# Cross attention of a decoder layer: the output's weights loaded and split in sixteen single pieces instead of four groups of four

## The chip, the cores and the metric

The kernel runs on one core of a Trainium2 chip. The metric is the device time in microseconds (us). The kernel before has three runs: 1482.58, 1488.05 and 1488.45 us, median 1488.05. One more execution was profiled, with a span of 1484.0 us.

A core has five engines that work side by side, each with its own queue of instructions: TensorE (PE, matrix products; PEld is its weight load), VectorE (DVE), ScalarE (ACT), GpSimd (POOL) and SyncE (SP), which here issues most of the DMA transfers. An engine takes its instructions in order; where one waits, all behind it on that engine wait too. PE's clock can be throttled: the profile shows the granted clock, 1.00 at full speed.

## The reference, cut to what matters

A decoder layer for 16 batches of 100 tokens, width 512, in float32:

```
x = layernorm(x + self_attention(x))                 # 16 heads, causal
x = layernorm(x + cross_attention(x, ctx))           # the change lies here
x = layernorm(x + moe(x))                            # top 2 of 8 experts, projection, rms norm

# cross attention: 16 heads of 128, 4 heads of keys and values, 361 encoder tokens a batch
q = rmsnorm((x @ Wq + bq) by heads) * qn_w
k = rmsnorm((ctx @ Wk + bk) by heads) * kn_w         # each serves four heads of q
v = (ctx @ Wv + bv) by heads
p = softmax(q k^T / sqrt(128) + mask)
cross_attention = (p v, heads side by side) @ Wo     # Wo: 2048 x 512
```

## The kernel before

**Pairs.** Every float32 array that enters a product is held as a pair, a high part [...] and a low part, the rest. `split` (L120 to L127) makes one: a cast of the high part on ACT (L124) and a subtraction of the low part on DVE or POOL (L127). `mm3` (L129 to L133) is one product of pairs in three matmuls, whose lines L131, L132 and L133 appear in the profile for all products.

**Weights.** The arena `WH`, `WL` has eight slots of 512x512 pairs. `load_unit` (L194) fills one through `split_rows` (L185 to L190): for each of four pieces of 128x512 (256 KB) it takes a stage tile (a ring of three, tag `f`), issues a DMA on SP that is kept in program order, casts on ACT and subtracts on POOL. The output's weights Wo take four slots (`wo_slot = (3, 7, 0, 4)`), one for each group of four heads, in tiles that the profile calls `f_wo`; they are first used with the last batch, by `d_part`.

**The stages.** Self attention in groups of four batches; a stage that makes the queries of the cross attention and writes them to DRAM (`qd`); the cross attention; its output product with the router; the experts, with tokens sorted by expert into tiles, gathered by indirect DMAs (`xs`, a ring of five), transposed on PE (`pte`), multiplied, and written back (`ysd`).

**The cross attention's loop.** It runs over 64 items, a batch b and a group of heads g, in the order b*4 + g. An item of group g does, in the program's order:
- for g = 0, 1, 2 the keys' and values' products of one chunk of the next batch's encoder tokens (`kv_project`: `pk`, `ks`, `pv`), and the split of the next chunk of the encoder tokens (`cf` to `cT`);
- `x_load` of the queries of the item after next (`qf`, on SP; split by ACT and POOL);
- for g = 1, 2, 3 the transposes of a chunk of the next batch's keys (`kv_turn`: `ptk`, `kT`);
- in turn: the next item's four heads of scores (`x_scores`: product `s`, bias and maximum on DVE, the exponential `p` on ACT, the sum's inverse on DVE, the scaling of `p` on POOL), the three transposes of its own probabilities (`x_turn`: `ptp`, split into `pT_h` by ACT and `pT_l` by DVE), and the products with the values (`x_attend`: `av`), the third of them one item late;
- behind the last of these, the output `o` of the item before on ACT (L720) and its write to DRAM (`od`, L725, on SP).

At the end of the items with g = 1 of batches 2, 5, 8 and 11 stands one `load_unit` of Wo, four pieces in a row:

```python
        if g == 1 and b in (2, 5, 8, 11):
            load_unit(f"wo_{b // 3}", wo_slot[b // 3], Wo4[b // 3])
```

**What sets the order.** The program is built in a tile context with a planner that simulates a timeline and orders each engine's instructions by it, so they do not follow the program's text strictly; DMAs marked with `keep_in_program_order` keep theirs among each other. An edit in one place can so move instructions in another.

Of the kernel before, what the change touches and what calls it, by code (L numbers as in the profile page):

```python
# [17 lines left out]
B, S, D = 16, 100, 512  # batches, tokens of a batch, model width  # L18
T = B * S
KC = D // 128  # chunks of the model width  # L20
NH = 16  # heads of both attentions
HD1 = D // NH  # head width of the self attention
SE = 361  # encoder tokens of a batch
SP = SE + 1  # the same, even
NKV, HD2 = 4, 128  # key/value heads and head width of the cross attention
GR = NH // NKV
CH = [(0, 128), (128, 128), (256, SE - 256)]  # chunks of the encoder tokens
NE = 8  # experts
GB = 4  # batches of a token group
NG = B // GB  # L30
GT = GB * S
TT = [(t, min(128, T - t)) for t in range(0, T, 128)]  # tiles of all tokens
# [5 lines left out]
def pieces(t0, n):  # L38
    """The batches that tokens t0 to t0 + n lie in: (batch, its token, offset, count)."""
    out, t = [], t0  # L40
    while t < t0 + n:
        b, r = divmod(t, S)
        m = min(S - r, t0 + n - t)
        out.append((b, r, t - t0, m))
        t += m
    return out


class Pair:
    """A float32 array as the exact sum of two that float32r holds."""  # L50
# [12 lines left out]
def tile_decoder_layer(  # L63
# [29 lines left out]
    # Exp and Ln of one table serve both attentions.  # L93
# [26 lines left out]
    def split(dst, src, high=None, low=None):  # L120
        """dst, a pair, from src."""
        high, low = high or nc.scalar, low or nc.vector
        if high is nc.scalar:
            nc.scalar.copy(dst.h, src)  # L124
        else:
            high.tensor_copy(dst.h, src)
        low.tensor_tensor(dst.l, src, dst.h.bitcast(FP), ALU.subtract)  # L127

    def mm3(out, a, b, start, stop):  # L129
        """The product of two pairs, to float32's accuracy."""  # L130
        nc.tensor.matmul(out, a.h, b.h, start=start, stop=False)  # L131
        nc.tensor.matmul(out, a.h, b.l, start=False, stop=False)  # L132
        nc.tensor.matmul(out, a.l, b.h, start=False, stop=stop)  # L133
# [5 lines left out]
    def rsqrt(v, p, n, name, p_=None):  # L139
        """1 / sqrt(v), from the activation tables, with one Newton step."""  # L140
# [33 lines left out]
    # Eight slots of 512 rows by 512 columns, each a pair: weights, and what fits  # L174
    # beside them.
# [6 lines left out]
    def slot_of(s):  # L182
        return Pair(WH[:, s], WL[:, s])

    def split_rows(dst, src, name, high=None, low=None):  # L185
        """Weights from DRAM into a pair, by rows."""
        for k in range(KC):
            f = stage.tile([128, D], FP, name=f"f_{name}_{k}", tag="f")
            tc.keep_in_program_order(nc.sync.dma_start(f, src[:, k]))
            split(dst[:, k], f, high, low or nc.gpsimd)  # L190
# [44 lines left out]
    def chunk(n, c, queue=None):  # L235
        """Weights from DRAM, 128 columns (of queries or keys) or rows (of values)."""
        cc = slice(c * 128, (c + 1) * 128)
        chunks.append(n)
        p, bufs = (w1, 2) if len(chunks) % 5 > 2 else (stage, 3)
        f = p.tile([128, KC, 128], FP, name=f"f_{n}_{c}", tag="f", bufs=bufs)  # L240
        if n == "v":
            f = f.rearrange("p k n -> p (k n)")
            part, dst = src[n][:, c], units["wv_s"][:, c]
        else:
            part, dst = src[n][:, :, cc], units[f"w{n}_s"][:, :, cc]
        (queue or nc.sync).dma_start(f, part)
        return dst, f
# [7 lines left out]
    # Keys of four heads, each in its own block of rows and of columns.  # L255
# [8 lines left out]
    # Added to negated scores: zero up to the diagonal, BIG past it.  # L264
# [35 lines left out]
    def self_q(g, c):  # L300
# [3 lines left out]
        # The scores come out negated and scaled.  # L304
# [71 lines left out]
    def self_attend(g, c, r):  # L376
# [3 lines left out]
        # Of each head's rows only its own columns are its output.  # L380
# [48 lines left out]
    LA = 3  # items that scores are ahead by  # L429
    extra = {}  # what comes with an item  # L430
# [77 lines left out]
    # Both norms' weights and the negated scale of the scores.  # L508
# [107 lines left out]
    # Six pairs of values and two of queries, in slots 1 and 5.  # L616
# [87 lines left out]
    def x_attend(b, g, i):  # L704
# [13 lines left out]
        # The weights of a token sum to one: the values' bias comes last.  # L718
# [27 lines left out]
    TAIL = 3  # tiles whose parts come by weights, not by tiles  # L746
# [12 lines left out]
    def d_part(i, among={}):  # L759
        """A part of the output's product; others' products are among its own."""  # L760
        t, g = parts[i]
        n = TT[t][1]
        if g == 0:
            # The scores' banks are free by the time that those of the first wait.
# [28 lines left out]
    HEAD = 1  # parts with a group of heads of the last batch  # L793
    d_i = ExitStack()
    for i, (b, g) in enumerate(order):
# [34 lines left out]
        if g == 1 and b in (2, 5, 8, 11):  # L830
            load_unit(f"wo_{b // 3}", wo_slot[b // 3], Wo4[b // 3])
# [13 lines left out]
    # Small products: logits, ranks, counts, tokens of slots, their experts.  # L845
# [30 lines left out]
    def d_logits(t):  # L876
        """The products of the router with a tile, to go among longer ones."""
# [15 lines left out]
    # An expert's tokens in order, 128 to a tile of slots. The tiles of slots come in  # L893
    # the order in which their first tokens do, but the first EARLY of those that the
    # tokens of the first CUT tiles fill come before the others.
    URGENT = 1000
    I32, HF = mybir.dt.int32, mybir.dt.float16
    NSL = NE + (2 * T - NE) // 128  # tiles of slots: enough for any choice
    CUT, EARLY = NT - 4, 11
    # At the cut at most NE - 1 tiles' worth of choices lies in tiles not full.  # L900
# [9 lines left out]
    # Whole numbers below 2 ** 11 are in float16 where products take them.  # L910
    # Expert numbers less NE, negative ones.
# [5 lines left out]
    # Ones where the partition's number comes before the column's.  # L917
# [11 lines left out]
    # lower[e, i] is one where i is less than e, on all partitions.  # L929
# [31 lines left out]
    def by_128(dst, src, name):  # L961
        """The whole part of src / 128."""
# [5 lines left out]
    def table(name, shape, dt=FP):  # L968
        """A table of shape, first after partitions the tiles."""
# [3 lines left out]
    def choose(a, b):  # L973
        """The two experts of each token of tiles a to b, and its ranks in them."""
# [4 lines left out]
        for j in range(2):  # L979
            # The largest value of each token, and the first place that has it.  # L980
# [19 lines left out]
        if b == NT:  # L1000
            # The last tile's tokens past the end choose none.
# [17 lines left out]
        if b in (CUT, NT):  # L1019
            # The choices that come before each tile of tokens.  # L1020
# [26 lines left out]
        # What the tokens give to their slots: the tile's expert, by its first slot,  # L1047
# [7 lines left out]
        # and their numbers.  # L1055
# [11 lines left out]
    def settle(a, b):  # L1067
        """The tiles of slots of the choices of tiles a to b."""
# [6 lines left out]
        # Tiles of slots that an expert has before each tile of tokens.  # L1075
# [4 lines left out]
        # One where it opens another.  # L1080
# [5 lines left out]
        def before_it(these, till, less, name):  # L1086
            """How many of these come before each."""
# [28 lines left out]
        # That one's place among all tiles of slots.  # L1116
        new = before_it(opn, opened, EARLY if a else 0, "new")
        if a == 0:
# [6 lines left out]
            # new less those of the first EARLY that come before it, negated,  # L1125
# [3 lines left out]
            # or first, if it is itself of those.  # L1129
# [6 lines left out]
        # The place of the one before it.  # L1136
# [7 lines left out]
        # The tile of slots of a choice, by its rank.  # L1144
# [18 lines left out]
    def slots(a, b, upto):  # L1163
        """Of tiles a to b of slots: the tokens, and where the weights lie."""
# [69 lines left out]
    early = [1, 2, 5, 6]  # slots that are free already  # L1234
# [117 lines left out]
    # Tiles of tokens from REST on come after the last product, from LATE on also  # L1352
    # the gathers for them.
    REST, LATE = 6, 8
    # When the tiles before LATE are turned to, by tiles of slots.
    TURN = (19, 20, 21, 22, 24, 26, 28, 30)
    BEHIND = 2  # products that the last norms come after

    def upto(t):
        """Tiles of slots among which are all that the tokens of tile t are in."""  # L1360
        # At most NE of the tiles so far are not full at the cut.
# [93 lines left out]
    # Roots taken together: of tiles in the first norm, of tiles in the second.  # L1455
# [16 lines left out]
    def root(j, t, of=V2):  # L1472
        """What to take the root of for tile t in norm j, or its reciprocal root."""
# [8 lines left out]
    def f_first(t):  # L1482
        """The first norm of tile t, and what the second takes."""
# [3 lines left out]
        # The first norm's result and x2, both times the root s: the second norm  # L1487
        # drops s, but for its share of v.
# [62 lines left out]
    def roots(v, m, name):  # L1551
        """Of v's first m columns the root of four times it, of the others 1 / sqrt."""
# [6 lines left out]
        # A Newton step for each.  # L1559
# [15 lines left out]
    def newton(v, name):  # L1575
        """1 / sqrt(v): from a guess by v's exponent, three Newton steps."""
# [130 lines left out]
```

## Time and profile before

| what | value |
|---|---|
| runs | 1482.58, 1488.05, 1488.45 us (median 1488.05) |
| profiled execution, span | 1484.0 us |
| mean granted clock of PE | 0.972 |
| PE, DVE, ACT, POOL busy | 94%, 69%, 55%, 49% |
| DMA, mean rate | 108 GB/s |
| loads of f_wo | 16, on SP at 582.8 to 949.4 us, to landing 2.6 / 4.6 / 5.9 us (min / median / max) |
| casts of f_wo on ACT (L124) | 16, median 622 ns; ACT waited for the DMA in 7 of them, 8.2 us |
| subtracts of f_wo on POOL (L127) | 16, median 1276 ns; POOL waited for ACT in 3 of them, 1.5 us |

How to read it: "busy" is the time in which an engine worked on an instruction. A line of a timeline has start, length (of a run of x instructions), engine, line of the kernel, operation, output<-input, shape, and in brackets how long the engine had been idle before it and what ended that. A line of a table of stretches has start:end and length, the busy time of PE, of its weight loads, of DVE, ACT and POOL with the counts of instructions, then the granted clock, the share of the DMA engines' time and GB/s. A batch's stretch is taken from its third-group score product to that of the next batch, which is a fixed place in the loop.

### The profile page before, as it was taken

The page shows a single profiled execution, that of the slowest core. Times are in us where ns is not written, and L with a number is a line of the kernel's source. Part 1 is how long each engine was busy: PE and PEld are TensorE (multiplying, and loading weights), DVE is VectorE, ACT ScalarE, POOL GpSimd, SP SyncE. Part 2 cuts the span into 40 slices and gives each one's busy share as a digit, 9 for nine tenths or more (in the row PEclk, how much of TensorE's full clock was granted, in tenths as well). Part 3 has the DMA queues.
Part 4 walks back from the last instruction along what each step waited for, and adds up shares of the span by engine and source line. Part 5 has one row for each costly group of instructions (what it writes and reads, how often), then busy time and mean ns, then how long its engine had stood idle before and what let it go on. Part 6 is the DMA issues. An engine that isn't in the chain of part 4 may idle for free.

```text
span 1484.0 us, 24770 instructions
## 1 busy us (share of the span) xinstructions
PE 1391.4 (94%) x7248; PEld 1139.8 (77%) x7248; DVE 1018.2 (69%) x3523; ACT 813.3 (55%) x2164; POOL 731.9 (49%) x853
## 2 busy tenths in 40 slices
PE   7999999999999999999999999999999898798985
PEld 6777786788877888788788788788887676576763
DVE  5775766677676777777777677677745558752698
ACT  5766877444444566566666566566654233332453
POOL 6455545534424555455655555555544444442643
PEclk9999999999999999999999999999999999899997
DMA  4011015456544222122322322321435645666774
GB/s 130 34 46 62 22 36 145 144 142 118 125 97 92 74 65 80 44 64 64 89 61 64 87 63 63 93 60 45 99 107 142 207 164 159 191 213 184 253 232 146
DMA packets 197875, 159.77 MB, mean 108 GB/s; under 512 B 133322, under 2 KB 152878, under 8 KB 197742
## 3 DMA queue, kind: packets, MB, share of 16 engines
q1 hardware_dynamic: 187904, 137.83, 33.7%
q0 software_dynamic: 4576, 14.95, 3.3%
q10 hardware_dynamic: 5262, 5.41, 1.3%
q8 instruction: 60, 0.98, 0.3%
q14 instruction: 73, 0.60, 0.1%
HBM read 107.16 MB, written 50.99 MB: 107 GB/s over the span
## 4 chain that ended last, share of the span: by engine, by line
PE 67%; DVE 17%; DMA 7%; issue 4%; ACT 3%; POOL 1%; SPq 1%; DVEq 0%; POOLq 0%; ACTq 0%
PE pv L131 4%; PE pv L132 4%; PE pv L133 4%; PE pq L131 4%; PE ptp L700 4%; PE pq L132 4%; PE pq L133 3%; PE s L131 3%; PE s L133 3%; PE s L132 3%; PE pk L131 3%; PE pk L133 3%; PE pk L132 3%; DVE ksq L639 2%; PE av L383 2%
## 5 line engine op out<-in xcount | busy, mean ns | idle before, releaser
L692 POOL TENSOR_SCALAR p<-p,sums 100x361 f32<-100x361 f32 x256 | 146.7, 577 | 107.7 <-DVE sums L691 88.7
L679 DVE CUSTOM_DVE_ANT_0 p<-s,nmask 100x361 f32<-100x361 f32 x256 | 133.5, 527 | 73.6 <-PE s L133 71.5
L690 ACT ACTIVATE p<-p,nm 100x361 f32<-100x361 f32 x256 | 153.4, 602 | 47.2 <-DVE nm L679 44.1
L127 DVE TENSOR_TENSOR pT_l<-ptp,pT_h 128x400 fp32r<-128x400 f32 (+1 forms) x192 | 107.4, 567 | 58.3 <-ACT pT_h L124 58.1
L124 ACT CAST pT_h<-ptp 128x400 fp32r<-128x400 f32 (+1 forms) x192 | 91.5, 488 | 33.4 <-PE ptp L700 32.8
L700 PE MATMUL ptp<-ident,p 100*128 100x100 f32 (+1 forms) x768 | 108.2, 253 | 0.1
L700 PEld LDWEIGHTS ptp<-ident,p 100*128 100x128 f32 (+1 forms) x768 | 95.9, 152 | 15.5 <-POOL p L692 4.2
L127 POOL TENSOR_TENSOR cT_l<-cf,cT_h 128x512 fp32r<-128x512 f32 (+1 forms) x48 | 54.4, 1134 | 97.2 <-ACT cT_h L124 95.9
L133 PE MATMUL acc<-WH,ot_l 128*128 128x512 f32 (+1 forms) x208 | 86.2, 415 | 8.4 <-DVE ot_l L127 5.4
L131 PE MATMUL acc<-WH,ot_h 128*128 128x512 f32 (+1 forms) x208 | 85.8, 413 | 3.5 <-ACT ot_h L124 3.5
L127 POOL TENSOR_TENSOR WL<-qf,WH 128x400 fp32r<-128x400 f32 x64 | 67.3, 1051 | 43.5 <-ACT WH L124 39.7
L131 PE MATMUL s<-kT_h,WH 128*100 128x362 f32 x256 | 88.7, 357 | 0.0
L131 PE MATMUL av<-pT_h,WH 128*128 128x400 f32 (+1 forms) x192 | 76.7, 400 | 8.2 <-ACT pT_h L124 8.2
L132 PE MATMUL acc<-WL,ot_h 128*128 128x512 f32 (+1 forms) x208 | 84.4, 406 | 0.0
L133 PE MATMUL s<-kT_h,WL 128*100 128x362 f32 x256 | 84.1, 329 | 0.0
L132 PE MATMUL s<-kT_l,WH 128*100 128x362 f32 x256 | 83.7, 327 | 0.0
L131 PE MATMUL pq<-WH 128*128 128x512 f32 (+1 forms) x208 | 82.3, 396 | 0.1
L132 PE MATMUL pq<-WL,WH 128*128 128x512 f32 (+1 forms) x208 | 81.6, 394 | 0.5 <-POOL WL L127 0.5
L551 POOL TENSOR_TENSOR qs<-qs,r_q 128x512 f32<-128x512 f32 (+1 forms) x52 | 54.3, 1075 | 54.5 <-DVE r_q L155 25.5
L131 PE MATMUL pv<-WH,cT_h 128*128 128x512 f32 (+1 forms) x192 | 80.3, 418 | 0.8 <-DVE WL L127 0.8
L639 DVE CUSTOM_DVE_ANT_0 ksq<-ks 128x128 f32<-128x128 f32 (+1 forms) x192 | 78.3, 408 | 2.4
L360 POOL TENSOR_TENSOR p<-p,rinv 100x400 f32<-100x400 f32 x64 | 54.2, 855 | 51.8 <-DVE rinv L359 37.3
(349 smaller groups left out, 4407.3 us busy)
## 6 DMA issues: line engine op xcount, KB each, us to landing
qf<-qd SPq DMA_DIRECT2D x64, 200.0 KB, 2.6
of<-od SPq DMA_DIRECT2D x48, 256.0 KB, 3.5
cf<-in_ctxT SPq DMA_DIRECT2D x16, 722.0 KB, 4.2
eb<-in_expert_b SPq DMA_DIRECT2D x32, 256.0 KB, 3.8
ysd<-xs SPq DMA_DIRECT2D x32, 256.0 KB, 4.1
f_e<-in_expert_w SPq DMA_DIRECT2D x30, 256.0 KB, 4.5
f_wq<-in_Wq SPq DMA_DIRECT2D x16, 256.0 KB, 4.0
f_wo<-in_Wo SPq DMA_DIRECT2D x16, 256.0 KB, 4.6
```

Of the source, the lines that this page charges most:

```text
L124: nc.scalar.copy(dst.h, src)
L127: low.tensor_tensor(dst.l, src, dst.h.bitcast(FP), ALU.subtract)
L131: nc.tensor.matmul(out, a.h, b.h, start=start, stop=False)
L132: nc.tensor.matmul(out, a.h, b.l, start=False, stop=False)
L133: nc.tensor.matmul(out, a.l, b.h, start=False, stop=stop)
L360: nc.gpsimd.tensor_tensor(p, p, rinv.unsqueeze(2).to_broadcast([S, 4, S]), ALU.mult)
L551: nc.gpsimd.tensor_tensor(qr[:, hs, :], qr[:, hs, :], rs[:n, hs].unsqueeze(2).to_broadcast([n, GR, HD2]), ALU.mult,)
L639: nc.vector.tensor_tensor_reduce(out=sq[:n], in0=kr[:, h, :], in1=kr[:, h, :], scale=1.0, scalar=0.0, op0=ALU.mult, op1=ALU.add, accum_out ...
L679: nc.vector.tensor_tensor_reduce(out=p, in0=sc[:, :SE], in1=nmask, scale=1.0, scalar=BIG, op0=ALU.add, op1=ALU.min, accum_out=nm,)
L690: nc.scalar.activation(p, p, AF.Exp, bias=nm, scale=-1.0, accum_out=sh)
L692: nc.gpsimd.tensor_scalar(p, p, sh, 1.0, ALU.mult, ALU.mult)
L700: nc.tensor.transpose(pt[:n, h, :], probs[h][:, c0 : c0 + n], ident[:S, :S])
```

## The change

The condition on g and b goes. A table `wo_rows` names sixteen items, every third one from item 8 to item 53, each with one piece m; a new function `load_row` does for one piece what `split_rows` does for four. m // 4 is the group of heads (the slot), m % 4 the piece in it. Item i is batch i // 4 with g = i % 4, so the pieces stand at g = 0, 3, 2, 1 in turn. The transfers, the casts and the subtracts are as many and as large as before.

```diff
     wo_slot = (3, 7, 0, 4)
+    wo_rows = {8 + 3 * m: m for m in range(NKV * KC)}
+
+    def load_row(name, src, slots_, m):
+        u, k = divmod(m, KC)
+        units[name] = slot_of(slots_[u])
+        f = stage.tile([128, D], FP, name=f"f_{name}_{k}", tag="f")
+        tc.keep_in_program_order(nc.sync.dma_start(f, src[u][:, k]))
+        split(units[name][:, k], f, nc.scalar, nc.gpsimd)
+
     for i, (b, g) in enumerate(order):
...
-        if g == 1 and b in (2, 5, 8, 11):
-            load_unit(f"wo_{b // 3}", wo_slot[b // 3], Wo4[b // 3])
+        if i in wo_rows:
+            load_row(f"wo_{wo_rows[i] // KC}", Wo4, wo_slot, wo_rows[i])
```

The rest of the diff takes out comments and docstrings. With the new places the planner also orders some instructions of the experts' stage differently: the products that count the tokens of each expert come one product later, and the transposes of several tiles of tokens (`pte`) and the gathers behind them come earlier. Lines behind the new function are ten further down.

## The prediction

> **What bounds the kernel now.** I read the page's shares of busy time first, then the cross attention cut at each batch's score product of its third group of heads (the table of stretches), then the chain of waits and each engine's timeline around one of the four loads. The page:
>
> ```profile
> span 1484.0 us, 24770 instructions
> PE 1391.4 (94%) x7248; PEld 1139.8 (77%) x7248; DVE 1018.2 (69%) x3523; ACT 813.3 (55%) x2164; POOL 731.9 (49%) x853
> ```
>
> TensorE sets the pace. The change lies in the cross attention, so what it can give is read there. Each row is start:end and length in us, the busy time of PE, weight loads, DVE, ACT and POOL with their counts, the granted clock, the DMA share and GB/s:
>
> ```profile
> 525.49:563.55 38.06, 37.81 (x219) 32.38 (x218) 28.46 (x109) 24.81 (x68) 19.73 (x28) 1.00 0.26 64
> 563.55:608.41 44.86, 41.48 (x220) 34.97 (x218) 30.85 (x110) 26.60 (x72) 24.69 (x32) 0.92 0.29 77
> 608.41:646.48 38.07, 37.82 (x219) 32.36 (x218) 28.48 (x110) 24.82 (x68) 19.73 (x28) 1.00 0.27 64
> 684.59:726.21 41.62, 38.45 (x219) 32.42 (x218) 30.66 (x109) 26.60 (x72) 24.66 (x32) 1.00 0.33 84
> 802.40:847.36 44.96, 41.52 (x219) 34.99 (x218) 30.43 (x109) 26.69 (x72) 24.68 (x32) 0.92 0.31 77
> 923.57:967.23 43.66, 40.00 (x219) 33.75 (x218) 30.34 (x109) 26.68 (x72) 24.72 (x32) 0.96 0.31 80
> ```
>
> A batch without a load takes 38.08 with PE 99% busy. The four with a load (4 more casts on ACT, 4 more subtracts on POOL: x68 to x72, x28 to x32) take 6.78, 3.54, 6.88 and 5.58 more: **22.8 us in all, the most that the change could take away here.** PE's own busy time grows where the clock is below 1. At half clock for 6.83, 0, 6.83 and 3.41 us (the lost clock times the length) half of that is lost: 8.5 us. The other 14.3 is plain waiting, about 3.6 a group, and the chain and the timelines show how it comes about:
>
> ```profile
> 581.82 0.91 SPq L725 DMA_DIRECT2D od<-o  x2
> 582.78 1.49 SPq L189 DMA_DIRECT2D f_wo<-in_Wo  x3
> ...
> 582.78 4.50 DMA f_wo<-in_Wo
> ...
> 587.30 0.62 ACT L124 CAST WH<-f_wo 128x512 fp32r<-128x512 f32 x1 [1.85 <-DMA f_wo<-in_Wo]
> ...
> 596.02 0.45 PE L132 MATMUL av<-pT_l,WH 128*128 128x400 f32 x1 [1.18 <-DVE pT_l L127]
> 598.07 0.57 PE L131 MATMUL av<-pT_h,WH 128*128 128x400 f32 x1 [1.06 <-ACT pT_h L124]
> ```
>
> The load is issued on SP directly behind the writes of o (od), which wait for the end of an item (a batch and a group of heads). It lands 4.5 us later, but ACT works in order and has its cast next, so it stands 1.85 us with everything behind it, then casts pieces between its exponentials; DVE and at last PE wait. The half clock begins some 0.5 us after these two gaps.
>
> **The change, part by part.** *The work is the same:* 16 loads, 16 casts at 622 ns, 16 subtracts at 1276 ns, now one of each with items 8, 11, ... 53. Nothing on PE is added. ACT is busy 25 of 38 us in a plain batch, POOL 20, SP less, so 16 x 0.62 = 10 us of ACT and 16 x 1.28 = 20 us of POOL have room on average; without that cover these sums would be the cost.
>
> *The wait of the first piece is not removed, it is had sixteen times.* In the changed order of instructions each load still stands directly behind the od writes, ahead of a load of queries (qf), on SP; each cast stands only some 3 us of ACT's work behind the same point. What I cost is one piece in a plain batch's timeline, put where the order has it. Landing is od's end plus 4.5 (first pieces of the four groups: 4.52, 4.26, 4.63, 4.62). Issuing a piece takes SP 0.43, by which qf is late; qf is for the item after next, so nothing waits. Behind the waiting cast on ACT are exponentials and pT_h; for these DVE (pT_l, ks) and then PE's av, ptp and pk wait. The four positions in a batch, four pieces each:
> - Items of g=0: ACT would reach the cast at 574.98, 695.55, 813.4, 935.0; the data land at 576.1, 696.6, 815.0, 936.15. With the cast, less the room before pk needs its bank: 0.8, 0.75, 1.3, 0.8 = 3.65.
> - g=3 (row below): od is issued at 641.94 to 642.85, the piece lands at 647.4; ACT is free at 645.19, so it stands 2.2 and casts 0.6. pT_h, due at 646.37, comes at about 648.5, and POOL's 1.28 lies ahead of the next p. PE loses about 2.2: x4 = 8.8.
> - g=2: two pieces ahead of the third pT_h, 1.35 and 1.9, two behind it, 0.7 each = 4.65.
> - g=1: reached at 668.2, 786.05, 907.16, 1027.1, landed at 669.7, 788.3, 909.2, 1028.6; less the room at pk: 0.3, 1.15, 0.9, 0.35 = 2.7.
>
> ```profile
> 641.94 0.91 SPq L725 DMA_DIRECT2D od<-o  x2
> ...
> 644.57 0.63 ACT L124 CAST cT_h<-cf 128x512 fp32r<-128x512 f32 x1 [0.29 <-PE pv L132]
> ...
> 646.37 0.47 ACT L124 CAST pT_h<-ptp 128x400 fp32r<-128x400 f32 x1
> ```
>
> Sum of waits: 19.8, against 14.3 before: **5.5 worse**. Bounds: 5 if the room downstream takes most of each (0.3 a piece), 29 if each costs the 1.8 that the first of a group stood.
>
> *The clock.* Before, groups cost 8.5 here. [...] gaps of 1.18 and 1.06 within 3 us were enough, in three of four groups. [...] by the row the six larger pieces (g=3 and two of g=2) are doubtful. At 1.7 a trip (half of 3.41) none to ten trips cost 0 to 17; I take two or three, 4, nearer the single gaps of before that tripped nothing (the 684.59 row at 1.00). **4.5 better.**
>
> [...] a DVE operation on 128x4 values took 1.28 alongside a subtract of f_wo:
>
> ```profile
> 595.88 1.28 DVE L171 TENSOR_SCALAR v_k<-kss 128x4 f32<-128x4 f32 x1
> ...
> 595.87 1.26 POOL L127 TENSOR_TENSOR WL<-f_wo,WH 128x512 fp32r<-128x512 f32 x1
> ```
>
> [...] DVE is 75% busy in a batch, and PE waits only where pT_l or ks is next. I keep it inside the waits above.
>
> *The experts' stage.* Nothing is edited there, but the planner orders it anew: the routing products go one product later, and the transposes of the tiles of tokens (pte), with the gathers behind them, several places sooner. Before, PE waits there on a ring of five gathered tiles:
>
> ```profile
> 1330.00:1350.00 20.00, 15.44 (x67) 11.90 (x66) 6.61 (x10) 5.68 (x10) 3.79 (x4) 0.91 0.67 212
> ...
> 1339.42 1.09 PE L1206 MATMUL pte<-ident,xs 128*128 128x128 f32 x4 [3.20 <-DMA xs<-x2d,idx]
> ...
> 1410.00:1430.00 20.00, 19.56 (x97) 15.51 (x96) 19.36 (x55) 9.06 (x18) 7.95 (x8) 1.00 0.86 256
> ```
>
> The first row has 4.6 us of PE idle and 0.9 of lost clock (9% of 20, halved); the gathers of tiles 13 to 15 come 3 to 5 us sooner in the new order, and later PE is 98% busy, so what is gained is kept. All of it would be 5.5, plus 2 for the wait at tile 19. I take **4 better**; from 8 better to 2 worse (the later routing products hold up the first tiles).
>
> Sum: +5.5 - 4.5 - 4 = -3 against the profiled 1484.0, so 1481 as a profile. The median of the runs is 1488.05, 4.05 above that span, and the three runs spread over 5.9, of which the profile lies in the lower part. Against the median the sum is **1485**.
>
> **The rivals.**
> 1. *Pieces trip the clock* (the other side). A wait of 2 us per piece halves the clock for a window or two, as a group does. Place: batches with a g=3 piece; price 3.4 (two windows) in each of four, and 1.7 in four more: 20 in place of 4, so 1485 + 16 = 1501. For it: three of four groups tripped. Against: they had two gaps over 1 and further ones. From 1495.5 - 1485 + 4 = 14.5 us of lost clock, some 8 windows, the kernel is measurably slower.
> 2. *PE's queue and the rooms absorb single pieces.* ACT's wait of 1 to 2 is made good before PE needs pT: 0.3 a piece, 5 in all, no trip: -14.3 + 5 - 8.5 = -18, with -4 elsewhere: 1466. For it: ACT is 35% free and its room returns with every item; the group at 684.59 cost only 3.54 for four. Against: PE has 0.25 us of idle time in 38, and pT is made just in time.
> 3. *Only the place moves*: pieces cost together what groups do (22.8), and the experts' stage gives nothing: 1488.
>
> **How the numbers follow.** A measurement tells about 0.5%, 7.4 us, from no change: 1480.6 to 1495.5 is the same. Chances: main case 0.40 (own range 1477 to 1492, its two unknowns being the clock 0 to 10 and the experts 0 to 8), rival 1 0.12, rival 2 0.30, rival 3 0.18. Faster: all of rival 2 and a third of the main case, 0.43; the bound's other side takes most of rival 1, 0.10. Same 0.47. The range 1465 to 1497 leaves out the far ends of rivals 1 and 2.
>
> **What would show it.** Right: ACT waits on f_wo in nearly all of 16 casts, together 20 us or more against 8.2 before (7 of 16); batches with a piece 39 to 41 long, g=3 ones the longest; granted clock at 1.00 in most; the wait before tile 13's transpose shorter. Wrong: batches of 38.1 to 38.5 throughout (rival 2), or four and more at 0.96 and below (rival 1).

## The result: 0.4% faster, and the profile after

The changed kernel takes 1479.28 us (median of six runs, 1472.23 to 1484.90) against 1485.53 for the kernel before beside it: a ratio of 0.9958, interval 0.9938 to 0.9979. On another chip the same pair gave 0.9981 (0.9963 to 0.9999). The forecast was 1485 with 1465 to 1497, and no change beyond 0.5% as the likeliest outcome. The time came out inside the range; the sum that led to it did not come out term by term, and that is what the experiments are about.

The page of the changed kernel, profiled execution:

```profile
span 1479.0 us, 24756 instructions
PE 1385.8 (94%) x7248; PEld 1135.1 (77%) x7248; DVE 1010.7 (68%) x3523; ACT 812.2 (55%) x2164; POOL 733.5 (50%) x853
```

Batches 2, 3, 4, 6, 9 and 12 of the cross attention, cut as before (start:end and length, busy time of PE, weight loads, DVE, ACT, POOL, granted clock, DMA share, GB/s):

```profile
562.98:601.01 38.03, 37.71 (x220) 32.44 (x218) 27.99 (x110) 24.30 (x66) 21.16 (x29) 1.00 0.31 77
601.01:642.86 41.85, 39.94 (x220) 33.82 (x218) 29.18 (x110) 26.49 (x72) 22.25 (x30) 0.96 0.28 64
642.86:681.45 38.59, 38.29 (x220) 32.53 (x218) 28.25 (x109) 25.12 (x69) 20.97 (x29) 1.00 0.29 69
719.47:759.45 39.98, 38.09 (x219) 32.36 (x218) 29.30 (x109) 26.23 (x72) 22.30 (x30) 1.00 0.27 68
836.01:881.38 45.37, 41.77 (x219) 34.97 (x218) 28.96 (x111) 26.59 (x72) 22.23 (x30) 0.92 0.24 60
957.89:1000.75 42.86, 40.32 (x219) 33.94 (x218) 29.03 (x111) 26.60 (x72) 22.23 (x30) 0.96 0.26 63
```

The cut is, put exactly, at the third score product of a batch's first group of heads, which PE makes during the item before. So a piece at the end of an item with g=3 falls into the next batch's stretch. Where four batches paid before, now twelve have a piece in them, and four of these (3, 6, 9, 12, the ones with a g=3 and a g=2 piece) pay nearly everything. Batches whose piece stands at g=0 (the first row) pay nothing.

The answer for the tile f_wo, and the three queues around the first piece at g=3:

```profile
L124 ACT CAST WH<-f_wo x16: 617/620/626, 575.7 to 1023.9; 128x512 fp32r<-128x512 f32 x16
...
  DMA f_wo<-in_Wo: 24.5, 16
```
```profile
597.90 0.50 SPq L800 DMA_DIRECT2D f_wo<-in_Wo  x1
...
601.89 0.62 ACT L124 CAST WH<-f_wo 128x512 fp32r<-128x512 f32 x1 [2.16 <-DMA f_wo<-in_Wo]
...
603.01 0.47 ACT L124 CAST pT_h<-ptp 128x400 fp32r<-128x400 f32 x1
...
603.53 0.45 PE L131 MATMUL av<-pT_h,WH 128*128 128x400 f32 x1 [1.28 <-ACT pT_h L124]
604.14 0.60 PE L132 MATMUL av<-pT_l,WH 128*128 128x400 f32 x1 [0.16 <-DVE pT_l L127]
```

Each of the sixteen casts makes ACT wait for its landing, 24.5 us in all (7 casts and 8.2 us before). At g=3 the cast comes just ahead of a pT_h, whose ptp PE had made by 601.23, and PE stands 1.28 and 0.16 us.

**An account for all runs.** The names are those of the experiments below. "Excess" is what batches 1 to 13 take over 38.08 us each. The trace shows the half clock (0.50) in stretches of 3.41 or 6.83 us, counted here as one or two windows; in before and after, matmuls of pv follow each other there at 0.43 us (median) in place of 0.23, and a window is counted as half of its length lost, 1.71. The rest of the excess is direct waiting. "Rest" is from batch 15's mark to the end of the execution. "Order" says which of the two orders of the experts' stage the build has.

| kernel | excess | half-clock windows (lost) | direct | ACT waited on f_wo | order | rest | ratio to before (95%) |
|---|---|---|---|---|---|---|---|
| before | 22.9 | 5 (8.5) | 14.4 | 8.2 | before | 390.7 | |
| after | 19.1 | 4 (6.8) | 12.3 | 24.5 | after | 390.1 | 0.9958 (0.9938-0.9979) |
| after_again | 18.6 | 3 (5.1) | 13.5 | 25.7 | after | 395.4 | 0.9981 (0.9963-0.9999) |
| early | 15.1 | 1 (1.7) | 13.4 | 24.6 | after | 395.3 | 0.9973 (0.9960-0.9987) |
| at01 | 17.7 | 4 (6.8) | 10.9 | 23.8 | before | 387.7 | 0.9980 (0.9958-1.0002) |
| at23 | 27.5 | 3 (5.1) | 22.4 | 29.4 | after | 393.7 | 1.0049 (1.0032-1.0066) |
| poolcast | 8.4 | 0 | 8.4 | 0 (POOL: 31.3) | after | 392.6 | one run |
| pin | 6.1 | 0 | 6.1 | 12.3 | near after | 391.7 | 0.9947 (0.9929-0.9965) |
| early_pin | 6.5 | 1 (1.7) | 4.8 | 0 | before | 392.3 | 0.9932 (0.9908-0.9955) |
| group_early | 19.2 | 6 (10.2) | 9.0 | 0.6 | before | 395.2 | 0.9996 (0.9980-1.0012) |
| group_dve | 4.8 | 0 | 4.8 | 0.4 | its own | 392.2 | 0.9908 (0.9876-0.9939) |
| before_dve | 11.6 | 2 (3.4) | 8.2 | 8.0 | after | 395.1 | 0.9939 (0.9918-0.9961) |
| after_dve | 19.3 | 2 (3.4) | 15.9 | 25.2 | after | 389.3 | 0.9985 (0.9961-1.0009) |
| best13 | 1.2 | 0 | 1.2 | 0 | before | 395.1 | 0.9866 (0.9835-0.9897) |

Excess and rest come from one profiled execution each, the ratios from up to twenty timed ones; the rest alone varies by 7.7 us over these executions. The two do not agree to the microsecond: against the kernel before, pin loses 16.8 us of excess and is timed 7.9 us faster, early_pin 16.4 and 10.1, group_dve 18.1 and 13.7, best13 21.7 and 20. The profiled execution of pin is the second fastest of 20 and that of early_pin the fastest of nine, so their excess may flatter them. Only the changed kernel was profiled twice (19.1 and 18.6).

### The profile page after: what moved, and what is told of

The parts are those of the page before. It is cut to its first block, busy times and chain, and to the rows that moved or that the text cites. A ratio compares the mean times of both kernels' runs of the same rounds, so it can differ in the third digit from the quotient of the medians.

```text
span 1479.0 us, 24756 instructions
## 1 busy us (share of the span) xinstructions
PE 1385.8 (94%) x7248; PEld 1135.1 (77%) x7248; DVE 1010.7 (68%) x3523; ACT 812.2 (55%) x2164; POOL 733.5 (50%) x853
## 5 line engine op out<-in xcount | busy, mean ns | idle before, releaser
L700 PEld LDWEIGHTS ptp<-ident,p 100*128 100x128 f32 (+1 forms) x768 | 95.6, 151 | 13.5 <-POOL p L692 2.3
L131 PE MATMUL pk<-WH,cT_h 128*128 128x512 f32 (+1 forms) x192 | 78.2, 407 | 0.2
```

The costliest lines, as they stand in the source:

```text
L700: nc.tensor.transpose(pt[:n, h, :], probs[h][:, c0 : c0 + n], ident[:S, :S])
```

## The experiments

**Is the wait for the landing what a piece costs?** First, the load one item earlier:

```diff
         if i in wo_rows:
-            load_row(...)                  # load, cast, subtract
+            split_row(wo_rows[i])          # cast, subtract
+        if i + 1 in wo_rows:
+            fetch_row(wo_rows[i + 1])      # load
```

> The changed kernel with one thing moved: the load of each piece is issued one item (6 to 14 us) before its cast; casts and subtracts stay at the same items, and the experts' stage has the changed kernel's order. Theory (the wait for the landing on ACT is what a piece costs): ACT waits on f_wo for less than 2 us in all (24.5 in the changed kernel), the batches' excess over 38.08 falls from 19.2 us to 0 to 3, no half clock in the cross attention, about 1462 us. Rival (the cast and the subtract themselves are in the way[...]): excess stays at 12 or more, 1472 us or more.

ACT waited as long as ever, so the experiment did not do what it was made for:

```profile
L124 ACT CAST WH<-f_wo x16: 617/620/626, 565.7 to 1011.3; 128x512 fp32r<-128x512 f32 x16
...
  DMA f_wo<-in_Wo: 24.6, 16
```

The first cast is now at 565.7 in place of 575.7: the planner moved it along with its load, apparently again to where it takes the data to have landed. An excess over 12 is here no evidence for the rival, since neither condition was tested. So the cast had to be held too:

```diff
-        split(units[name][:, k], WF.pop(m), nc.scalar, nc.gpsimd)
+        dst, f = units[name][:, k], WF.pop(m)
+        tc.keep_in_program_order(nc.scalar.copy(dst.h, f))
+        nc.gpsimd.tensor_tensor(dst.l, f, dst.h.bitcast(FP), ALU.subtract)
```

> As the run with early loads, but each cast is also held, in ACT's order, behind the last exponential of its item, so that the load runs 6 to 14 us ahead of its cast; the experts' stage comes in the order of the kernel before. Theory (the wait for the landing on ACT is what a piece costs): ACT waits on f_wo for less than 2 us in all, the batches' excess over 38.08 is 0 to 4 us, no half clock in the cross attention, 18 to 22 us less than the kernel before. Rival (the casts and subtracts themselves are in the way): excess 10 or more, at most 12 us less.

No wait is left, and 19 us of excess become 6.5, of which one half-clock window is 1.7. That is above the 0 to 4 without a half clock that I had expected, and the timed gain is 10.1 us and not 18 to 22. The direct 4.8 lies in the g=2 pieces (batches 3, 6, 9 and 12: 1.1 each beside the window), and there it is no landing:

```profile
628.65 1.27 POOL L801 TENSOR_TENSOR WL<-f_wo,WH 128x512 fp32r<-128x512 f32 x1
628.66 1.28 DVE L171 TENSOR_SCALAR v_k<-kss 128x4 f32<-128x4 f32 x1
...
629.98 0.20 ACT L143 ACTIVATE a_k<-v_k 128x4 f32<-128x4 f32 x1 [2.29 <-DVE v_k L171]
...
630.86 0.45 PE L131 MATMUL av<-pT_h,WH 128*128 128x400 f32 x1 [1.06 <-ACT pT_h L124]
```

DVE's v_k (made from the keys' square sums; ACT's a_k is its logarithm) takes at most 0.47 us in the loop save in these four places, where it takes 1.28 or 1.29 beside the piece's subtract on POOL. The a_k waits for it, and pT_h stands behind a_k on ACT.

The hold alone, with the loads as late as in the changed kernel:

> The changed kernel with one thing added: each cast is held, in ACT's order, behind the last exponential of its item; the loads are issued as late as in the changed kernel. The cast moves back by two to nine places on ACT (g=2 not at all). Theory: ACT waits less, 4 to 14 us in place of 24.5, above all at g=3 and g=1, excess 6 to 12 against 19.2, 5 to 12 us less than the changed kernel. Rival (the cast's own time): no change, excess 17 to 21.

Excess 6.1, ratio 0.9947, with 12.3 us of waiting left on ACT. So the sum of ACT's waits isn't the measure. Of the eight waits left, six cost PE at most 0.41 us each; the two directly ahead of a pT_h (2.14 and 1.99 us) made it stand 1.46 and 1.31. What costs is a waiting cast close ahead of a pT_h. Loading early on top of the hold gains nothing clear of noise (0.9932 against 0.9947, with intervals that overlap), so the cast's place is what matters most, and the planner had it too early. Beside the changed kernel, pin was 4.7 us faster, just under the 5 to 12 expected.

**The queue.** The cast on POOL in place of ACT (`split(..., nc.gpsimd, nc.gpsimd)`):

> The changed kernel with the cast of each piece on POOL in place of ACT, at the same items; the experts' stage in the changed kernel's order. Theory (the harm comes through ACT's queue, where pT_h and the exponentials stand behind the cast): ACT waits on no f_wo, POOL waits instead, about 20 us in all, with the scaling of p behind it, which has some room: excess 5 to 12. Rival (a wait costs the same in any queue on the way to PE): excess 17 or more, since POOL's part grows by another cast.

Excess 8.4, no half clock: POOL waits longer than ACT ever did (31.3, where I had expected about 20) and PE loses less. So most of the harm came through ACT's queue, as far as one timed run tells.

**The place.** Pieces at g=0 and g=1 of eight batches, then at g=2 and g=3:

```diff
-    wo_rows = {8 + 3 * m: m for m in range(NKV * KC)}
+    wo_rows = {8 + 4 * (m // 2) + m % 2: m for m in range(NKV * KC)}    # at01
+    wo_rows = {10 + 4 * (m // 2) + m % 2: m for m in range(NKV * KC)}   # at23
```

> The changed kernel with other items: the sixteen pieces stand at the ends of items with g=0 and g=1 of batches 2 to 9, loaded as late as before; the experts' stage comes in the order of the kernel before. Theory (a late landing costs only where PE soon needs what stands behind the cast; g=0 costs 0 and g=1 about 0.4 in the changed kernel): ACT still waits 15 to 25 us in all, excess 0 to 5 us, no half clock, 1462 to 1466 us. Rival (each wait costs about the same wherever it stands, 1.2 us a piece): excess about 19, 1479 us. If the new order of the experts' stage was worth something (4 us in the prediction), that stage is longer here than in the changed kernel by it.

> The changed kernel with other items: the pieces stand at the ends of items with g=2 and g=3 of batches 2 to 9, with the experts' stage in the changed kernel's order. Theory (places where PE has no room): 8 x 1.4 for g=3 and 8 x 1.2 for g=2 of direct waits = 21, and a half clock of 3.4 us (1.7 lost) in most of the eight batches, 8 to 15: excess 29 to 36, 1489 to 1497 us. Rival (place does not matter): excess about 19, 1479 us.

The second is slower than the kernel before, with twice the direct waits of the first (22.4 against 10.9): place matters. Its direct waits were near the 21 expected, but only 5.1 us of half clock came in place of 8 to 15, so its excess of 27.5 fell short of 29 to 36. The first missed its 0 to 5 by far and came out near the rival's 19 (17.7). Its trace shows why: in batch 4 the g=0 cast waits 0.40 us and costs PE nothing, yet the output o of that item comes 1.90 us later than in a plain batch; the g=1 load stands behind o's write on SP, and its cast then waits 2.30. One piece makes the next one late. What a place costs alone can't be added up for neighbours.

**Where did the groups' cost come from?** If it was the landing, then groups loaded early should cost little. The kernel before, with three loads of a group one item earlier and its casts held:

```diff
+        if g == 0 and b in (2, 5, 8, 11):
+            for k in range(KC - 1):
+                fetch_row(b // 3, k)
         if g == 1 and b in (2, 5, 8, 11):
-            load_unit(f"wo_{b // 3}", wo_slot[b // 3], Wo4[b // 3])
+            ...                            # fetch the fourth; held casts; subtracts on POOL
```

> The kernel before, still with four groups of four pieces; the first three loads of a group are issued one item earlier, the casts are held behind the last exponential of their item, the fourth piece comes as before. Three casts stand directly behind each other on ACT. Theory (it was the landing and not the grouping that cost): ACT waits on f_wo for less than 3 us, excess 0 to 8 us against 22.8, no half clock, 14 to 22 us less than the kernel before. Rival (four pieces at once crowd ACT and POOL): 1.9 us of casts in a row hold up pT_h as long as the landing did, excess 14 or more, at most 8 us less.

ACT's waits are gone (0.6), and nothing is gained: excess 19.2, in the rival's range, and ratio 0.9996. The theory that the landing was the groups' whole cost falls here. DVE, POOL and PE in its first group:

```profile
591.66 2.84 DVE L639 CUSTOM_DVE_ANT_0 ksq<-ks 128x128 f32<-128x128 f32 x1
...
591.45 1.05 POOL L127 TENSOR_TENSOR cT_l<-cf,cT_h 128x420 fp32r<-128x420 f32 x1
592.47 0.58 POOL L692 TENSOR_SCALAR p<-p,sums 100x361 f32<-100x361 f32 x1
...
593.08 1.27 POOL L846 TENSOR_TENSOR WL<-f_wo,WH 128x512 fp32r<-128x512 f32 x1
...
596.51 0.45 PE L132 MATMUL av<-pT_l,WH 128*128 128x400 f32 x1 [3.10 <-DVE pT_l L127]
```

DVE's square sum of the keys, 0.29 us as a rule, took 2.84: it began 0.2 us after one POOL instruction had begun, POOL went on from one into the next, and it ended 0.15 us after the subtract of f_wo. PE waited 3.10 for the pT_l behind it. It comes once in each of the four groups (2.83 or 2.84), and in the kernel before too (1.59 to 1.63, four times), where the same row of POOL's instructions stands beside it:

```profile
592.93 1.63 DVE L639 CUSTOM_DVE_ANT_0 ksq<-ks 128x128 f32<-128x128 f32 x1
...
592.72 0.60 POOL L692 TENSOR_SCALAR p<-p,sums 100x361 f32<-100x361 f32 x1
...
593.37 1.05 POOL L127 TENSOR_TENSOR WL<-qf,WH 128x400 fp32r<-128x400 f32 x1
```

So early loads removed the landing and at the same time made this wait longer. In the changed kernel no ksq is over 1.19.

How this reaches PE in the kernel before can be read from its trace, and it sets the prediction's reading right. In a group, PE's first gap stands behind the cast that waited for the landing. The next two, the ones that the prediction showed (1.18 and 1.06), do not: one comes behind the long ksq, the other behind ACT's a_k, which waited for the v_k of 1.28 us:

```profile
589.33 0.45 PE L131 MATMUL av<-pT_h,WH 105*128 105x400 f32 x1 [0.79 <-ACT pT_h L124]
...
597.20 0.21 ACT L143 ACTIVATE a_k<-v_k 128x4 f32<-128x4 f32 x1 [3.36 <-DVE v_k L171]
...
597.55 0.87 ACT L124 CAST pT_h<-ptp 128x400 fp32r<-128x400 f32 x2
```

All four groups have these three gaps. Together they are 3.8 us behind the landing, 3.8 behind the ksq and 4.2 behind the v_k.

The new theory: the long ksq (2.84 and 1.63 in place of 0.29) comes from the row of POOL's instructions without a gap that the subtracts make. It is tested by moving the subtracts to the other engine:

```diff
-                nc.gpsimd.tensor_tensor(dst.l, f, dst.h.bitcast(FP), ALU.subtract)
+                nc.vector.tensor_tensor(dst.l, f, dst.h.bitcast(FP), ALU.subtract)
```

> The run with early groups, with one more thing moved: the subtracts of the four pieces go to DVE in place of POOL. There, four times, DVE's square sum of the keys (ksq, 0.29 us as a rule) took up to 2.84 us beside a row of POOL's instructions, and PE then waited 3.1. Theory [...]: ksq never over 1.3 us, excess 19.2 down to 4 to 11, half clock 0 to 3.4 us lost in place of 5.1, although DVE has 4 x 4 subtracts more. Rival (the three casts in a row on ACT): excess 15 to 21, since the casts stay as they are and DVE gets fuller.

19.2 becomes 4.8, with no half clock and no ksq over 1.30, although the three casts stay in a row and DVE has more to do. So grouping costs little once neither the landing nor POOL's row of subtracts is in the way. The same edit to the two kernels of the case (`low=nc.vector`), with nothing else edited; in the changed kernel an excess under 12 would say that single subtracts on POOL cost too:

> The kernel before with one thing changed: the subtracts of the sixteen pieces go to DVE in place of POOL; groups, loads and casts stay where they are, and ACT still waits for the first piece of a group (8 us in all). The experts' stage comes in the changed kernel's order. Theory (most of a group's cost is POOL's row of subtracts[...]): ksq under 1.4 us (1.63 before), half clock in none or one of the four groups, excess 6 to 14 us against 22.9. Rival (the landing wait at the head of a group is its cost, as the prediction had it): excess 18 to 23.

> The changed kernel with the same one thing changed: the sixteen subtracts go to DVE. Theory (single subtracts on POOL find DVE with room, ksq never over 1.2 us in the changed kernel; what a piece costs is the wait on ACT): ACT waits 22 to 27 us as before, excess 15 to 21 against 19.1 and 18.6. Rival [...]: excess under 12.

The kernel before falls from 22.9 to 11.6, its ksq to 1.19 at most and its v_k to 0.47; the half clock is left in two groups, one more than expected. The changed kernel stays at 19.3. One rival is left in part: with the subtracts on DVE the planner also put the pT_l that PE waits for ahead of two or three of the four ksq, so how much of the gain is that of the moved subtracts and how much this order's stays open. The two kernels have different costs: before paid POOL's rows of subtracts (and with them most of the clock's loss, 8.5 against 3.4) and four landings, after pays sixteen landings. Batches 2, 5, 8 and 11 of the kernel before with its subtracts on DVE, to be held against 44.86, 41.62, 44.96 and 43.66:

```profile
563.32:604.51 41.19, 39.55 (x220) 33.68 (x218) 30.96 (x114) 26.75 (x72) 20.50 (x28) 0.96 0.34 84
...
680.72:720.65 39.93, 38.34 (x220) 32.41 (x218) 30.61 (x114) 26.66 (x72) 20.56 (x28) 1.00 0.35 87
...
796.85:839.10 42.25, 39.66 (x220) 33.43 (x218) 31.01 (x113) 26.71 (x72) 20.50 (x28) 0.96 0.32 82
...
915.25:955.69 40.44, 38.20 (x220) 32.34 (x218) 31.01 (x114) 26.79 (x72) 20.52 (x28) 1.00 0.33 86
```

**A version that beats both.** Single pieces, loaded early, casts held, at g=1 and g=3 only:

```diff
-    wo_rows = {8 + 3 * m: m for m in range(NKV * KC)}
+    wo_rows = {9 + 2 * m: m for m in range(NKV * KC)}
```

> The run with early loads and held casts, with other items: one piece with each g=1 and each g=3 of batches 2 to 9, none with g=2, which cost 1.1 us a piece there (g=0 and g=3 nothing, g=1 0.15). Theory (a piece without a landing wait costs only where its cast stands ahead of a pT_h that PE needs): excess 1 to 3 us, no half clock, 20 to 22 us less than the kernel before in the cross attention. Rival (denser pieces crowd each other): excess as there, 5 to 8.

```profile
603.43:641.66 38.23, 37.89 (x219) 32.39 (x218) 28.64 (x110) 25.84 (x70) 22.18 (x30) 1.00 0.33 77
641.66:679.87 38.21, 37.93 (x220) 32.44 (x218) 28.61 (x109) 25.84 (x70) 22.14 (x30) 1.00 0.30 77
```

Two pieces in a batch cost 0.15 us. The time is 1465.44 us, ratio 0.9866: 20 us below the kernel before, against 21.7 of excess gone.

**Once more the changed kernel**, for how far one profile can be trusted:

> The changed kernel once more, beside the others on one chip, for a second trace. If the cross attention's cost is set by the order of instructions, direct waits come out as before (12.4 us, 24.5 us of waiting on ACT); the half clock (6.8 us lost) may differ by one or two windows of 1.7[...]. The experts' stage, from its first output product to the end, took 366.0 us here and 366.6 in the kernel before; other runs in the same two orders had 363.5 and 368.5 to 371.1, so I expect 366 to 371: no gain from the new order.

Cross attention as expected (18.6; direct waits 13.5, ACT's wait 25.7). The rest of the execution took 395.4 us in place of 390.1: the 5 us by which the first profile of after was shorter than that of before are no larger than what one kernel differs from itself there.

## Why the prediction was right

Its number was right by luck: three terms missed in ways that cancelled. Against the profile of before the sum was waits +5.5, clock -4.5, experts -4, together -3. Measured: waits -2.1 (14.4 to 12.3), clock -1.7 (8.5 to 6.8), the experts and the output's product -0.6, and -0.6 before the cross attention began: -5.0. Of its signs, ACT's sixteen waits came, but only one batch with a piece took 39 to 41 us (39.98); the others took 38.0 to 38.6 or 41.9 to 45.4.

- **"The wait of the first piece is not removed, it is had sixteen times": right.** 16 waits and 24.5 us, foretold as nearly all and 20 or more. Each load did stand behind the od writes, as the order had it.
- **The waits by position: too dear.** g=0 was put at 3.65 and costs 0 (38.03, 38.03, 38.09 and 38.05 for the four batches): ACT's instructions come up to 1.8 us late, but PE has products of the next batch in front of it, and the planner had moved what DVE does in between. g=1 was put at 2.7 and costs 1.4. g=3 and g=2 together were put at 13.45 and cost 10.9. Main term right in kind, 19.8 in place of 12.3 in size.
- **What the 14.3 before consisted of: wrong, and the real failing step.** "The other 14.3 is plain waiting ... the chain and the timelines show how it comes about" laid it to the landing, but the two gaps of PE that it showed stand behind DVE's ksq and v_k (8.0 us in the four groups, against 3.8 behind the landing). Take the landing away and 9.0 of direct waits is left, with all of the clock's loss; take POOL's subtracts away and direct waits fall to 8.2 and the clock's loss to 3.4. The rows that would have said so were quoted: v_k took 1.28 beside a subtract, and DVE's busy time rose from 28.46 to 30.85 us in a batch with a group although its instructions went only from 109 to 110. But "I keep it inside the waits" left this out of what the change removes. It removes what POOL's rows of subtracts cost, about half of the excess as far as before_dve tells (11.3 of 22.9), and gives back three landings for each it had.
- **The clock: direction right, size off.** 4 expected, 6.8 and 5.1 lost in two traces. The row was right in kind: four windows tripped, the first after gaps of 1.28 + 0.16 us. The "single gaps" of the 684.59 row were misread: that group has the same two gaps as the others (1.14 and 1.07), and the last section shows where they lay.
- **The experts' stage: wrong.** The step "later PE is 98% busy, so what is gained is kept" failed. Counted from the product acc_3 (the output product's fourth tile, ahead of the experts), tile 13's product begins 4.6 us sooner than before, as foretold, but tile 14's only 0.1: the wait for the gathered tile (3.20 before tile 13's transposes) is now 3.50 before tile 14's. Tile 23's begins 3.7 sooner; at the first projection only 0.3 is left, since between the two PE stands again:

```profile
1339.61 1.08 PE L1216 MATMUL pte<-ident,xs 128*128 128x128 f32 x4 [3.50 <-DMA xs<-x2d,idx]
...
1384.17 0.50 PE L131 MATMUL pp<-pw_h,cp_h 128*128 128x512 f32 x1 [3.08 <-issue]
...
1383.53 0.59 ACT L124 CAST cp_h<-ptc 128x512 fp32r<-128x512 f32 x1 [4.84 <-remote]
```

  Why ACT's cast came 6 us behind its input the trace does not show; it stays open. Over seven executions in the order of after the rest is 389.3 to 395.4, mean 393.1, over five in that of before 387.7 to 395.2, mean 392.2: no gain. The sum had a slip too: the 0.9 us of lost clock in its first row is about 1.8, since 9% of 20 us is already the loss.
- **The rivals.** Rival 1 (trips decide) did not come in the changed kernel, 4 windows against the 8 it needed. Nor did it in at23, which is slower by 0.5% through direct waits (22.4) with only three windows. Rival 2 (the rooms absorb) is true of g=0 and nearly of g=1 (1.4 for four), and of g=3 too once the cast is held; with the pieces at g=1 and g=3, loaded early and held, it is true of all (1.2 for sixteen). Rival 3 (22.8 and no gain from the experts) has the experts right and is 3.7 too high in the cross attention.

## What to carry to other kernels

A load's cast placed by a planner stands where the planner believes the data to have landed; look at the wait on the casting engine, and hold the cast behind work that surely takes longer, before changing how the loads are grouped. When a burst of work slows others down, ask of each engine in the burst whose instructions grow longer beside it: here the DMA was in the chain, but more of PE's waiting stood behind DVE's instructions that were held up beside POOL's row of subtracts (8.0 us against 3.8). Splitting a burst removes crowding and multiplies whatever each piece costs alone, so the two have to be costed apart.

## What the runs showed of the hardware

**DVE's instructions took longer beside POOL's, one of them through several in a row.** The longest ksq, 2.84 us in group_early where the median is 0.29, outlasted two whole POOL instructions (0.58 and 1.27 us) and most of a third (1.05) that followed each other with at most 0.03 us between. That is more than the one subtract of 1.28 in the prediction's row. With the subtracts on DVE no ksq took over 1.30 (group_dve). A v_k of 4 values in a row took 1.28 or 1.29 beside one subtract, in place of at most 0.48 elsewhere in the loop. By what means POOL's instructions hold up DVE's the traces do not show. A batch in which this falls just ahead of a pT_l or pT_h pays for it, with a group (1.06 us of PE's time) as with a single piece (1.06 in early_pin).

**The half clock came on one grid of 3.41 us, behind windows in which PE had stood.** The half-clock stretches of one execution's cross attention start a whole number of 3.4133 us apart: in before at 598.25, 837.18 and 960.06, 70 and 106 of them from the first; in after at 604.27, 839.79, 873.92 and 993.39, 69, 79 and 114 of them. The first of before begins 0.18 us behind its group's second gap, not the 0.5 of the prediction. Cut into these windows, the two traces have 355 at full clock from 478 to 1108 us. Seven of them were followed by a half-clock window, with 2.23, 1.84, 1.83, 1.75, 1.62, 1.44 and 1.31 us of idle time of PE in them. The others were not: five with 1.35, 1.28, 1.23, 1.14 and 1.02, and 343 with 0.90 at most. So in these two traces 1.44 us (42% of a window) was always enough, and 1.31 once where 1.35 was not. In the group that tripped nothing, an edge of this grid at 717.71 leaves 1.14 us of idle time in one window and 1.23 in the next, where the first group has 2.23 in one. That this spared it, and that the two executions of the changed kernel differ by a window (4 and 3) for such a reason, is my estimate from these figures.
